# One group for both halves of the masked scores, context two steps behind, and turned weights on one queue: a cross-attention block on one core

## Chip, core and metric

The kernel runs on one core of one Trainium2 chip. The metric is device time in microseconds (us) of one execution, as the median of several runs. One further execution was taken by the hardware profiler; its rows are what "the profile" and "the trace" mean here. The engines are TensorE (PE: matmuls; PEld: its weight loads), VectorE (DVE), ScalarE (ACT), GpSimd (POOL) and SyncE (SP, which here only issues transfers). ACT can issue transfers too; "SPq" and "ACTq" are those issues.

## What is computed

A block of a transformer for 128 sequences of 128 tokens with 256 features, all in fp32: cross-attention with 16 heads of 16 features against a second input of the same shape, a layer norm, a feed-forward part of width 1024, and a second layer norm. The mask lets token i see only the tokens j < i of the other input; the first token sees none, and its attention is zero.

```python
q = (query @ Wq + bq).reshape(b, s, H, 16).transpose(0, 2, 1, 3)
k = (key @ Wk + bk).reshape(b, s, H, 16).transpose(0, 2, 1, 3)
v = (values @ Wv + bv).reshape(b, s, H, 16).transpose(0, 2, 1, 3)
scores = einsum('bhqd,bhkd->bhqk', q, k) / sqrt(16)
scores = where(j < i, scores, -1e30)
attn = softmax(scores, axis=-1)
attn = attn.at[:, :, 0, :].set(0.0)
ctx = einsum('bhqk,bhkd->bhqd', attn, v).transpose(0, 2, 1, 3).reshape(b, s, 256)
x = layer_norm(query + ctx @ Wo + bo, ln1_g, ln1_b)
out = layer_norm(x + relu(x @ W1 + b1) @ W2 + b2, ln2_g, ln2_b)
```

`query` is the input x; `key` and `values` are both the second input.

## The kernel before

The 128 sequences are worked in 64 pairs (`NP` = 64); one pair `p` is 256 columns in most matmuls. The order of the work on every engine is the order in which the program issues it: nothing reorders it. So `step(p)` (L821), which is called for p = 2 to 62, is the schedule, and what stands before it (prologue, pairs 0 and 1) and behind it (epilogue, from L934) are written out by hand. A wait arises where an instruction needs a result, or a buffer that another still reads.

**Stages of one pair.** `tokens` turns the loaded blocks into feature-major tiles `xT` and `cT` (VectorE). `queries`, `keys`, `values` are projections (TensorE) that ACT copies out of PSUM: `qT`, `kT`, and the values into `vz` and `vd`. ACT's `values_out` also issues one transfer that moves half of the values to other partitions of `vd`.

`scores(p, hi)` (L312) is done twice for a pair. The mask makes a triangle, so the last 64 queries of a sequence ("high", `hi` = 1) go against all 128 tokens and the first 64 ("low", `hi` = 0) only against the first 64. Each call is 32 matmuls on tiles of 32 rows (two heads) by 64 columns: four row strips `r` by two halves `s` (the two sequences). In both calls every row strip writes a PSUM bank of its own, `sps[r // 2][.., r % 2, ..]`.

`mask` (VectorE, out of PSUM), `maximum` (VectorE reduces, POOL subtracts), `exponential` (ACT) and `sums` (VectorE adds up and takes reciprocals, POOL multiplies) make the softmax: in two halves of the heads, `ONE` and `TWO`, for high and in one piece, `ALL`, for low. The weights must then be turned, tokens onto partitions: `turn` (L381) transposes 32x32 blocks on VectorE into `tb`, three calls a pair, and `bring` (L394) moves the blocks to their partitions by sixteen transfers into `pT`, one for each (i, j). In `step` eight are issued by SyncE, and eight by ACT between the relus of the hidden layer:

```python
def share(f):
    nonlocal at
    n = NS * NS - at if f == FC - 2 else 0 if f == 0 or p == 2 else NS // 2
    bring(p, nc.scalar, range(at, at + n))
    at += n
```

`weigh` (L424) multiplies `pT` with the values into `pc`, `context` (L454) copies `pc` to `cxT` on ACT, `attention_out` (L458) is the output projection `po`. `attention_sum`, `attention_stats`, `norm1` are the first layer norm; `turn_x1` turns its result, by a VectorE transpose, four transfers out to DRAM and one back in, all on SyncE. `hidden` (L639) makes `ph`, two chunks of 128 a bank, and ACT's relus write `hT`; `second` (L660) makes `py`. `second_sum`, `stats`, `scale_and_shift`, `norm2`, `finish` and `store` are the second layer norm and the way out.

**Order in a step.** TensorE does in step p: high scores of p, `second` of p−3, `weigh` of p−1, low scores of p, `queries(p+1)`, `attention_out(p-1)`, `keys(p+1)`, `values(p+1)`, `hidden(p-2)`. So the context of a pair is made one step behind its scores.

**PSUM.** Eight banks: `ps_2` holds two pairs of banks (used for scores only), `ps_1` four single banks that all else takes in turn through `bank` (L209).

**Ends.** For pairs 0, 1 and 63 the weights, and for pairs 0 and 63 `x1`, are turned by TensorE (`turn_on_pe`, L406; `turn_x1_on_pe`), with ACT copying out of PSUM.

Of the kernel before, what the change touches and what calls it, by code (L numbers as in the profile page):

```python
# [19 lines left out]
def tile_cross_attention_block(  # L20
# [51 lines left out]
    ps_2 = ctx.enter_context(tc.tile_pool(name="ps_2", bufs=2, space=bass.MemoryType.PSUM))  # L72
    ps_1 = ctx.enter_context(tc.tile_pool(name="ps_1", bufs=4, space=bass.MemoryType.PSUM))

# [132 lines left out]
    bov_r = const.tile([P, D], F32, tag="bov_r", name="bov_r")  # L207

    def bank(name):  # L209
        return ps_1.tile([P, 512], F32, tag="ps1", name=name)  # L210

# [39 lines left out]

    def project(w, src, name):
        ps = bank(name)
        for m in range(KC):
            for k in range(KC):
                nc.tensor.matmul(  # L256
                    ps[:, m * TP : (m + 1) * TP], w[:, k, m * P : (m + 1) * P], src[:, k, :],
                    start=(k == 0), stop=(k == KC - 1),
                )
        return ps  # L260

    def queries(p):
        st = states[p]
        st["qT"] = proj.tile([P, KC, TP], F32, tag="qT", name=f"qT_{p}")
        pq = project(wq, st["xT"], f"pq_{p}")
        for m in range(KC):
            nc.scalar.activation(
                st["qT"][:, m, :], pq[:, m * TP : (m + 1) * TP], AF.Identity,
                bias=bqs_c[:, m : m + 1], scale=QSCALE,
            )  # L270

    def keys(p):
        st = states[p]
        st["kT"] = proj.tile([P, KC, 2, TP], F32, tag="kT", name=f"kT_{p}")
        pk = project(wk, st["cT"], f"pk_{p}")
        for m in range(KC):
            for e in range(2):
                nc.scalar.activation(  # L278
                    st["kT"][:, m, e, :], pk[:, m * TP : (m + 1) * TP], AF.Identity,
                    bias=bkh[:, m, e : e + 1], scale=half[:, e : e + 1],  # L280
                )

    def values(p):
        st = states[p]
        pv = st["pv"] = bank(f"pv_{p}")
        for s in range(2):
# [25 lines left out]
    def scores(p, hi):  # L312
# [20 lines left out]
        )  # L333
        st["nmx", hi] = small.tile([P, H], F32, tag=f"nmx{hi}", name=f"nmx{hi}_{p}")

    def mask(p, hi, t):
# [87 lines left out]
    def weigh(p):  # L424

        st = states[p]
        pT = st.pop("pT")
        pc = bank(f"pc_{p}")

# [28 lines left out]
    def attention_out(p):  # L458
        st = states[p]
        po = st["po"] = bank(f"po_{p}")  # L460
        for s in range(2):
# [31 lines left out]
    def attention_stats(p):  # L493
        stats(p, states[p]["t1"], 1)
        deviation(p, 1)
# [143 lines left out]
    def hidden(p, fs, between=None):  # L639
        st = states[p]  # L640
        if fs[0] == 0:
            st["hT"] = ffn.tile([P, FC, TP], F32, tag="hT", name=f"hT_{p}")
        for f in fs[::2]:
            ph = bank(f"ph_{p}_{f}")
            for i in range(2):
# [14 lines left out]
    def second(p, s, fs=range(FC)):  # L660
        st = states[p]
        if s == 0 and fs[0] == 0:
            st["py"] = bank(f"py_{p}")
        for f in fs:
# [143 lines left out]
    def load_ahead(p):  # L808
        if p % 2 == 0 and p + 4 < NP:
            load([p + 4, p + 5], "x")  # L810
        if p % 2 == 1 and p + 3 < NP:
            load([p + 3, p + 4], "c")
            load_tokens((p + 3) // 2)

# [5 lines left out]

    def step(p):  # L821
        nonlocal waiting
        if p > 2:
            load_ahead(p)
        scores(p, 1)
        mask(p, 1, 0)
        maximum(p, 1, ONE)
        if p > 2:
            second(p - 3, 0)
            mask(p, 1, 1)  # L830
            maximum(p, 1, TWO)
            exponential(p, 1, ONE)
            second(p - 3, 1)
            if p + 2 < NP:
                tokens(p + 2, "c")
        else:
            turn_x1_on_pe(0)
            turn_on_pe(1, 1, range(2))
            fold_norm1()
            add_b1()  # L840
            hidden(0, range(FC // 4))
            mask(p, 1, 1)
            maximum(p, 1, TWO)
            exponential(p, 1, ONE)
            low_scores(p)
            hidden(0, range(FC // 4, FC // 2))
            turn_on_pe(1, 1, range(2, 4))
            turn_on_pe(1, 0, range(2))
            hidden(0, range(FC // 2, 3 * FC // 4))
            tokens(3, "x")  # L850
            add_bo(1)
        summed = []
        sums(p, 1, ONE)
        exponential(p, 1, TWO)
        if p > 2:
            second_sum(p - 3)
            summed = [p - 3]
        else:
            tokens(3, "c")
            load_ahead(2)  # L860
            load_tokens(2)
            exponential(p, 0, ALL)
        sums(p, 1, TWO)


        weigh(p - 1)
        context(p - 1)
        if p > 2:
            scores(p, 0)
        if p == 3:  # L870
            scale_w1()
            nc.gpsimd.tensor_tensor(b1e_c, b1e_c, b1_c, ALU.add)
        queries(p + 1)
        if p > 2:
            mask(p, 0, 0)
            mask(p, 0, 1)
            maximum(p, 0, ALL)
        if p > 2:
            exponential(p, 0, ALL)
        else:  # L880
            sums(p, 0, ALL)
            add_bo(2)
        turn(p, 1, 0)
        turn(p, 1, 1)
        for q in waiting:
            finish(q)
        attention_out(p - 1)
        attention_sum(p - 1)
        if p > 2:
            sums(p, 0, ALL)  # L890
        else:
            turn(p, 0, 0)
            bring(p, nc.sync, range(NS * NS // 2))
        attention_stats(p - 1)
        if p + 2 < NP:
            tokens(p + 2, "x")
            if p == 2:
                tokens(p + 2, "c")
        if p > 2:
            turn(p, 0, 0)  # L900
            bring(p, nc.sync, range(NS * NS // 2))
        keys(p + 1)
        norm1(p - 1)
        turn_x1(p - 1)
        values(p + 1)
        values_out(p + 1)
        for q in waiting:
            store(q)
        add_bo(p + 1)
        if p == 2:  # L910
            residual1(0)
        residual1(p - 1)
        for q in summed:
            stats(q, states[q]["t2"], 2)
        for q in summed:
            scale_and_shift(q)
        at = NS * NS // 2

        def share(f):
            nonlocal at  # L920
            n = NS * NS - at if f == FC - 2 else 0 if f == 0 or p == 2 else NS // 2
            bring(p, nc.scalar, range(at, at + n))
            at += n

        hidden(p - 2, range(0 if p > 2 else 3 * FC // 4, FC), share)
        for q in summed:
            norm2(q)
        waiting = summed

    waiting = []  # L930
    for p in range(2, NP - 1):
        step(p)

    p = NP - 1  # L934
    scores(p, 1)
    mask(p, 1, 0)
    maximum(p, 1, ONE)
    second(p - 3, 0)
    mask(p, 1, 1)
    maximum(p, 1, TWO)  # L940
    exponential(p, 1, ONE)
    second(p - 3, 1)
    sums(p, 1, ONE)
    exponential(p, 1, TWO)
    second_sum(p - 3)
    sums(p, 1, TWO)
    weigh(p - 1)
    context(p - 1)
    scores(p, 0)
    mask(p, 0, 0)  # L950
    mask(p, 0, 1)
    maximum(p, 0, ALL)
    hidden(p - 2, range(FC // 2))
    exponential(p, 0, ALL)
    finish(p - 4)
    attention_out(p - 1)
    attention_sum(p - 1)
    sums(p, 0, ALL)
    attention_stats(p - 1)
    norm1(p - 1)  # L960
    turn_x1(p - 1)
    store(p - 4)
    residual1(p - 1)
    stats(p - 3, states[p - 3]["t2"], 2)
    scale_and_shift(p - 3)
    hidden(p - 2, range(FC // 2, FC))
    turn_on_pe(p, 1, range(4))

    p = NP - 1
    turn_on_pe(p, 0, range(2))  # L970
    norm2(p - 3)
    finish(p - 3)
    second(p - 2, 0)
    weigh(p)
    context(p)
    second(p - 2, 1, range(FC // 2))
    store(p - 3)
    attention_out(p)
    second(p - 2, 1, range(FC // 2, FC))
    attention_sum(p)  # L980
    attention_stats(p)
    second_sum(p - 2)
    hidden(p - 1, range(FC - 2))
    norm1(p)
    stats(p - 2, states[p - 2]["t2"], 2)
    turn_x1_on_pe(p)
    hidden(p - 1, range(FC - 2, FC))
    residual1(p)
    scale_and_shift(p - 2)
    hidden(p, range(FC // 2))  # L990
    second(p - 1, 0)
    hidden(p, range(FC // 2, FC))
    norm2(p - 2)
    finish(p - 2)
    store(p - 2)
    second(p - 1, 1)
    second_sum(p - 1)
    stats(p - 1, states[p - 1]["t2"], 2)
    deviation(p - 1, 2)
# [6 lines left out]
    for s in range(2):  # L1006
        py = bank(f"py_last_{s}")
        for f in range(FC):
# [49 lines left out]
```

## Time and profile before

| what | value |
|---|---|
| median of 3 runs | 1588.46 us (1586.27 to 1589.66) |
| span of the profiled execution | 1585.6 us |
| TensorE busy | 1573.8 us, 16514 matmuls |
| VectorE busy | 1370.8 us |
| POOL busy | 1281.4 us |
| ACT busy | 757.5 us |
| granted TensorE clock, 71.21 to 1457.53 us | 1.00 |
| busy share of the 16 DMA engines, same stretch | 0.60 |

The span runs from the first to the last instruction of the profiled execution; the runs are timed from outside. Busy times of different engines overlap each other. Matmuls are pipelined, so in a timeline a group's duration reaches into the next line: the distance between two starts is what a group holds TensorE for. In a timeline row stand start, duration, engine, line, operation, the tile written, `<-`, the tiles read, the shape and how many instructions were joined (x32); in square brackets follows idle time of the engine ahead of it and what ended it.

### The profile page before, as it was taken

Reading aid. Unit: us, or ns where it says so; the run is one execution under the profiler, and the core shown is the slowest. Engines: PE = TensorE matmul, PEld = TensorE weight load, DVE = VectorE, ACT = ScalarE, POOL = GpSimd, SP = SyncE. Lnnn points to the kernel's source line nnn. Section 1 sums busy time; section 2 is a strip of 40 time slices with the busy share of each in tenths; the row PEclk is TensorE's granted clock in tenths of the full one; section 3 lists DMA queues with packets and bytes.
Section 4 is the critical chain, followed back from the end, with each engine's and each line's share of the span. In section 5 each row is a group of like instructions: output and inputs, shape, how many; then the busy total and the mean of one; then the engine's idle time right before and its main releaser. Section 6 shows DMA issues by size and latency. Waiting matters only on the chain.

```text
span 1585.6 us, 41282 instructions
## 1 busy us (share of the span) xinstructions
PE 1573.8 (99%) x16514; PEld 1326.7 (84%) x16514; DVE 1370.8 (86%) x1989; ACT 757.5 (48%) x1500; POOL 1281.4 (81%) x1105
## 2 busy tenths in 40 slices
PE   9999999999999999999999999999999999999998
PEld 7788888888888888888888888888888888888887
DVE  7898988888888988898898988888889889889872
ACT  5555454444444454444444544444444455445442
POOL 7888888788787888888888888888888888888883
PEclk9999999999999999999999999999999999999999
DMA  9565665655656556556566565565555665664521
GB/s 199 115 137 128 140 147 121 150 122 130 151 127 141 138 123 157 136 123 149 127 137 148 127 149 130 117 160 128 138 134 126 152 147 121 144 137 108 127 78 34
DMA packets 479935, 210.12 MB, mean 133 GB/s; under 512 B 348672, under 2 KB 448256, under 8 KB 479744
## 3 DMA queue, kind: packets, MB, share of 16 engines
q1 hardware_dynamic: 371104, 134.29, 39.1%
q10 hardware_dynamic: 108640, 73.19, 18.0%
q8 instruction: 131, 2.15, 0.6%
q14 instruction: 60, 0.49, 0.1%
HBM read 70.00 MB, written 33.03 MB: 65 GB/s over the span
## 4 chain that ended last, share of the span: by engine, by line
PE 91%; DVE 3%; DMA 2%; POOL 1%; SPq 1%; ACT 1%; issue 1%; ACTq 0%; POOLq 0%; DVEq 0%
PE ph L647 26%; PE py L665 26%; PE pq L256 7%; PE po L463 7%; PE pk L256 6%; PE pv L288 6%; PE pss L322 6%; PE pc L444 3%; PE pc L434 2%; DMA pT<-tb 2%; SPq L402 1%; DVE su L372 1%; POOL sm L374 1%; DVE tb L387 0%; POOL sm L353 0%
## 5 line engine op out<-in xcount | busy, mean ns | idle before, releaser
L353 POOL TENSOR_TENSOR sm<-sm,nmx 128x1024 f32<-128x1024 f32 x192 | 364.2, 1898 | 118.6 <-DVE nmx L352 118.4
L647 PE MATMUL ph<-x1T,w 128*128 128x256 f32 x2048 | 453.6, 379 | 0.0
L665 PE MATMUL py<-w,hT 128*128 128x256 f32 x2016 | 453.0, 382 | 0.1
L665 PEld LDWEIGHTS py<-w,hT 128*128 128x128 f32 x2016 | 377.5, 190 | 73.4 <-issue 18.1
L374 POOL TENSOR_TENSOR sm<-sm,rs 128x1024 f32<-128x1024 f32 x192 | 364.2, 1898 | 90.1 <-DVE rs L373 84.1
L647 PEld LDWEIGHTS ph<-x1T,w 128*128 128x128 f32 x2048 | 388.7, 190 | 53.5 <-ACT x1T L632 0.5
L653 ACT ACTIVATE hT<-ph,b1e_c 128x256 f32<-128x256 f32 x504 | 208.7, 471 | 205.1 <-PE ph L647 99.2
L360 ACT ACTIVATE sm<-sm 128x1024 f32<-128x1024 f32 x192 | 201.1, 1054 | 203.9 <-POOL sm L353 195.6
L372 DVE TENSOR_REDUCE su<-sm 128x8 f32<-128x1024 f32 (+1 forms) x192 | 233.7, 1217 | 68.8 <-ACT sm L360 66.5
L341 DVE TENSOR_TENSOR sm<-pss,neg 128x1024 f32<-128x1024 f32 (+1 forms) x256 | 235.2, 940 | 51.1 <-PE pss L322 51.1
L387 DVE STREAM_TRANSPOSE tb<-sm 128x1024 f32<-128x1024 f32 x183 | 219.9, 1227 | 27.8 <-POOL sm L374 27.8
L352 DVE TENSOR_REDUCE nmx<-sm 128x8 f32<-128x1024 f32 (+1 forms) x192 | 234.3, 1220 | 6.6
L542 ACT ACTIVATE t<-t,nb,sd 128x256 f32<-128x256 f32 x124 | 67.7, 593 | 188.5 <-DMA pT<-tb 106.6
L256 PE MATMUL pq<-xT,wq 128*128 128x256 f32 x504 | 125.5, 392 | 0.0
L278 ACT ACTIVATE kT<-pk,bkh,half 128x256 f32<-128x256 f32 x252 | 120.6, 558 | 3.9 <-PE pk L256 3.8
L463 PE MATMUL po<-wo,cxT 128*128 128x256 f32 x512 | 121.1, 379 | 0.0
L288 PE MATMUL pv<-wv,cT 128*128 128x256 f32 x512 | 121.0, 379 | 0.0
L256 PE MATMUL pk<-cT,wk 128*128 128x256 f32 x504 | 119.2, 379 | 0.0
L322 PE MATMUL pss<-kT,qT 32*64 32x256 f32 (+1 forms) x4096 | 116.7, 334 | 0.0
L517 POOL TENSOR_TENSOR x1b<-x,g_r 128x512 f32<-128x512 f32 x64 | 81.5, 1273 | 34.9 <-DVE x L509 34.9
L463 PEld LDWEIGHTS po<-wo,cxT 128*128 128x128 f32 x512 | 97.2, 190 | 13.5 <-ACT cxT L456 0.3
L288 PEld LDWEIGHTS pv<-wv,cT 128*128 128x128 f32 x512 | 97.2, 190 | 13.2
(99 smaller groups left out, 1716.1 us busy)
## 6 DMA issues: line engine op xcount, KB each, us to landing
pT<-tb SPq DMA_DIRECT2D x488, 96.0 KB, 3.0
pT<-tb ACTq DMA_DIRECT2D x488, 96.0 KB, 2.7
out_dram<-t ACTq DMA_DIRECT2D x63, 256.0 KB, 2.5
xb<-in_x_dram SPq DMA_DIRECT2D x124, 128.0 KB, 4.5
cb<-in_ctx_dram SPq DMA_DIRECT2D x124, 128.0 KB, 4.3
x<-in_x_dram SPq DMA_DIRECT2D x31, 512.0 KB, 5.0
x1t<-tbx SPq DMA_DIRECT2D x248, 64.0 KB, 2.3
x1T<-x1t SPq DMA_DIRECT2D x62, 256.0 KB, 3.2
```

The lines of the kernel that those rows point to most:

```text
L256: nc.tensor.matmul(ps[:, m * TP : (m + 1) * TP], w[:, k, m * P : (m + 1) * P], src[:, k, :], start=(k == 0), stop=(k == KC - 1),)
L288: nc.tensor.matmul(pv[:, s * D : (s + 1) * D], st["cT"][:, k, s * P : (s + 1) * P], wv[:, k, :], start=(k == 0), stop=(k == KC - 1),)
L322: nc.tensor.matmul(sps[r // 2][s * HP : (s + 1) * HP, r % 2, m * 2 * n : (m + 1) * 2 * n].rearrange("p (e j) -> p e j", e=2), st["qT"][str ...
L341: nc.vector.tensor_tensor(st["sm", hi][:, part, :].rearrange("p (r n) j -> p r n j", r=2), st["sps", hi][t][:, :, : 4 * n].rearrange("p r ...
L352: nc.vector.tensor_reduce(nmx[:, part], sm[:, part, :], AX.X, ALU.max, negate=True)
L353: nc.gpsimd.tensor_tensor(sm[:, part, :], sm[:, part, :], nmx[:, part, None].to_broadcast([P, part.stop - part.start, n]), ALU.add,)
L372: nc.vector.tensor_reduce(su, sm[:, part, :], AX.X, ALU.add)
L374: nc.gpsimd.tensor_tensor(sm[:, part, :], sm[:, part, :], rs[:, :, None].to_broadcast([P, part.stop - part.start, n]), ALU.mult,)
L387: nc.vector.transpose(st["tb"][:, :, at : at + 256].rearrange("p j (n a) -> p n j a", a=32), st["sm", hi].rearrange("p h j -> p (h j)")[:, ...
L463: nc.tensor.matmul(po[:, s * D : (s + 1) * D], cxT[:, k, s, :], wo[:, k, :], start=(k == 0), stop=(k == KC - 1),)
L647: nc.tensor.matmul(ph[:, i * TP : (i + 1) * TP].rearrange("p (s i a) -> p s i a", s=2, a=32), w1[:, k, (f + i) * P : (f + i + 1) * P], st[ ...
L665: nc.tensor.matmul(st["py"][:, s * D : (s + 1) * D], st["hT"][:, f, s * P : (s + 1) * P], w2[:, f, :], start=(f == 0), stop=(f == FC - 1),)
```

## The change

High and low scores of a pair are issued together, in `scores_both`: eight groups of four tiles, with the low scores in one fixed pair of banks, `low`. Strips 0 and 1 share the first of them and strips 2 and 3 the second, at different offsets; `one` and `two` take the strips of a bank in opposite halves of the partitions. Ahead of the last eight low matmuls stands a tiny ACT copy from `low` into `hop`. `mask_low` masks all low scores in one instruction. The other single banks shrink to two; `queries`, `weigh` and `attention_out` use those, `second` too, `keys` and `values` share a pair, `hidden` takes a pair for its first half and `low` for its second. `hT` has one buffer instead of two.

In the new `step(p)`, called for p = 4 to 63, TensorE does `weigh(p-2)`, both scores of p, `queries(p+1)`, `attention_out(p-2)`, `keys(p+1)`, `values(p)`, `hidden(p-3)`, `second(p-3)`. The context is made two steps behind the scores. The sixteen transfers of `bring(p-1)` are all issued by SyncE, in one run. `third` and `fourth` are the steps for p = 2 and 3 (`fourth` weighs nothing); the last step issues half of `bring(62)` from ACT, and in the epilogue pair 63 is turned by `turn` and `bring` and `turn_x1` as the others are, not by TensorE.

```diff
-    ps_1 = ctx.enter_context(tc.tile_pool(name="ps_1", bufs=4, space=bass.MemoryType.PSUM))
+    ps_1 = ctx.enter_context(tc.tile_pool(name="ps_1", bufs=2, space=bass.MemoryType.PSUM))
+    ps_l = ctx.enter_context(tc.tile_pool(name="ps_l", bufs=1, space=bass.MemoryType.PSUM))
...
+    low = ps_l.tile([P, 2, 512], F32, tag="low", name="low")
+    turns = [0]
+
+    def single(name):
+        return ps_1.tile([P, 512], F32, tag="ps1", name=name)
+
     def bank(name):
-        return ps_1.tile([P, 512], F32, tag="ps1", name=name)
+        turns[0] += 1
+        return single(name) if turns[0] % 4 < 2 else low[:, turns[0] % 2]
...
+    hop = const.tile([HP, 2, 1], F32, tag="hop", name="hop")
+
+    def scores_both(p):
+
+        st = states[p]
+        sps = [pair(f"pss_{p}_{t}") for t in range(2)]
+        one = [(1, 1), (3, 1), (0, 0), (2, 0)]
+        two = [(1, 0), (0, 1), (3, 0), (2, 1)]
+        for tiles, hi, m in (
+            (one, 0, 0), (two, 1, 0), (one, 0, 1), (one, 1, 0),
+            (two, 1, 1), (one, 1, 1), (two, 0, 0), (two, 0, 1),
+        ):
+            n = P if hi else HP
+            for r, s in tiles:
+                strip, first = slice(32 * r, 32 * r + 32), s * P
+                rows = slice(s * HP, (s + 1) * HP)
+                at = m * 2 * n
+                if hi:
+                    to = sps[r // 2][rows, r % 2, at : at + 2 * n]
+                else:
+                    to = low[rows, r // 2, r % 2 * 4 * n + at : r % 2 * 4 * n + at + 2 * n]
+                nc.tensor.matmul(
+                    to.rearrange("p (e j) -> p e j", e=2),
+                    st["qT"][strip, m, first + hi * HP : first + hi * HP + HP],
+                    st["kT"][strip, m, :, first : first + n],
+                    start=True, stop=True,
+                )
+            if not hi and tiles is one and m == KC - 1:
+                nc.scalar.copy(hop, low[:HP, :, 2 * n : 2 * n + 1])
...
+    def mask_low(p):
+        nc.vector.tensor_tensor(
+            states[p]["sm", 0],
+            low.rearrange("p b (n j) -> p (b n) j", j=HP),
+            neg[:, 1, None, :].to_broadcast([P, H, HP]),
+            ALU.add,
+        )
...
-            st["hT"] = ffn.tile([P, FC, TP], F32, tag="hT", name=f"hT_{p}")
+            st["hT"] = ffn.tile([P, FC, TP], F32, tag="hT", name=f"hT_{p}", bufs=1)
         for f in fs[::2]:
-            ph = bank(f"ph_{p}_{f}")
+            if p == 0:
+                ph = bank(f"ph_{p}_{f}")
+            elif f < FC // 2:
+                if f == 0:
+                    st["ph"] = pair(f"ph_{p}")
+                ph = st["ph"][:, f // 2]
+            else:
+                ph = low[:, f // 2 - 2]
...
+    EVERY = range(NS * NS)
...
+    def fourth():
+        p = 3
+        load_ahead(p)
+        scores_both(p)
+        mask(p, 1, 0)
+        maximum(p, 1, ONE)
+        second(0, 0)
+        exponential(p, 1, ONE)
+        mask(p, 1, 1)
+        maximum(p, 1, TWO)
+        second(0, 1)
+        scale_w1()
+        mask_low(p)
+        maximum(p, 0, ALL)
+        queries(p + 1)
+        exponential(p, 1, TWO)
...
+        keys(p + 1)
+        second_sum(0)
...
+    def step(p):
+        last = p == NP - 1
+        load_ahead(p)
+        weigh(p - 2)
+        scores_both(p)
+        context(p - 2)
+        if p > 4:
+            second_sum(p - 4)
+        turn(p - 1, 1, 0)
+        turn(p - 1, 1, 1)
+        if p > 4:
+            residual1(p - 3)
+            finish(p - 5)
+            add_bo(p - 1)
+        mask(p, 1, 0)
+        maximum(p, 1, ONE)
+        if not last:
+            queries(p + 1)
+        if p > 4:
+            store(p - 5)
+        attention_out(p - 2)
+        mask(p, 1, 1)
+        maximum(p, 1, TWO)
+        exponential(p, 1, ONE)
+        turn(p - 1, 0, 0)
+        bring(p - 1, nc.sync, EVERY[: 8 if last else 16])
+        mask_low(p)
+        maximum(p, 0, ALL)
+        if not last:
+            keys(p + 1)
+        else:
+            bring(p - 1, nc.scalar, EVERY[8:])
+            states[p]["pkv"] = pair(f"pkv_{p}")
+        exponential(p, 1, TWO)
+        attention_sum(p - 2)
+        stats(p - 4, states[p - 4]["t2"], 2)
+        scale_and_shift(p - 4)
+        values(p)
+        values_out(p)
+        sums(p, 1, ONE)
+        exponential(p, 0, ALL)
+        attention_stats(p - 2)
+        sums(p, 1, TWO)
+        hidden(p - 3, range(FC))
+        norm2(p - 4)
+        sums(p, 0, ALL)
+        norm1(p - 2)
+        turn_x1(p - 2)
+        if p + 2 < NP:
+            tokens(p + 2, "x")
+            tokens(p + 2, "c")
+        second(p - 3, 0)
+        second(p - 3, 1)
+
+    third()
+    fourth()
+    for p in range(4, NP):
+        step(p)
     p = NP - 1
...
     weigh(p - 1)
     context(p - 1)
...
+    turn(p, 1, 0)
+    turn(p, 1, 1)
+    turn(p, 0, 0)
+    bring(p, nc.sync, EVERY[:8])
...
+    bring(p, nc.scalar, EVERY[8:12])
...
+    hidden(p - 2, range(FC // 2))
+    bring(p, nc.scalar, EVERY[12:])
...
-    turn_on_pe(p, 1, range(4))
...
-    turn_on_pe(p, 0, range(2))
...
-    turn_x1_on_pe(p)
...
+    turn_x1(p)
```

## The prediction

> **What bounds the kernel now.** I read the page from the top: busy shares, then the chain that ended last.
>
> ```profile
> PE 1573.8 (99%) x16514; PEld 1326.7 (84%) x16514; DVE 1370.8 (86%) x1989; ACT 757.5 (48%) x1500; POOL 1281.4 (81%) x1105
> PE 91%; DVE 3%; DMA 2%; POOL 1%; SPq 1%; ACT 1%; issue 1%; ACTq 0%; POOLq 0%; DVEq 0%
> ```
>
> TensorE is busy for 99% of the span and carries 91% of the chain. Between 71.21 and 1457.53 us it is busy 1385.01 of 1386.32 us. A change pays only by taking time from TensorE's own stream; a wait anywhere else that reaches TensorE costs in full. So next the timeline of TensorE for one pair (start, duration, operation, count).
>
> ```profile
> 760.16 7.07 PE L647 MATMUL ph<-x1T,w 128*128 128x256 f32 x32
> 767.16 1.12 PE L322 MATMUL pss<-kT,qT 32*64 32x256 f32 x32
> 768.21 7.17 PE L665 MATMUL py<-w,hT 128*128 128x256 f32 x32
> 775.31 0.43 PE L434 MATMUL pc<-pT,vd 128*32 128x64 f32 x16
> ...
> 776.79 0.69 PE L322 MATMUL pss<-kT,qT 32*64 32x128 f32 x32
> 777.41 1.99 PE L256 MATMUL pq<-xT,wq 128*128 128x256 f32 x8
> 779.25 1.89 PE L463 MATMUL po<-wo,cxT 128*128 128x256 f32 x8
> 780.97 1.89 PE L256 MATMUL pk<-cT,wk 128*128 128x256 f32 x8
> 782.70 1.89 PE L288 MATMUL pv<-wv,cT 128*128 128x256 f32 x8
> 784.42 7.07 PE L647 MATMUL ph<-x1T,w 128*128 128x256 f32 x32
> ```
>
> Starts are what to compare, since a duration overlaps the next line. One pair takes 784.42 − 760.16 = 24.26 us. High scores hold 768.21 − 767.16 = 1.05 and low scores 777.41 − 776.79 = 0.62, at two separate places.
>
> **The merged scores.** Eight plain 128x256 matmuls take 782.70 − 780.97 = 1.73, so 32 take 6.91. The 32 of ph, which end at scores, take 7.00; the 32 of py, which begin after scores and end at pc, take 7.10; pq, after scores, takes 1.84. Each change of tile shape therefore costs about 0.09 going out and 0.10 coming in. Today's step has four such changes from plain to narrow and back: into and out of high scores, into pc, and out of low scores. After the change pc and scores stand together: two remain.
> Inside a group, 32 matmuls of 256 columns take 1.05 and 32 of 128 columns 0.62. If a + 2b = 1.05 and a + b = 0.62, then b = 0.43 and a = 0.19 is a fixed part. One group of both is a + 3b = 1.48.
> New in it is `hop`, an ACT copy that the last eight low matmuls wait for. The twelve high matmuls behind the first low ones cover 12 × 1.05 / 32 = 0.39. PE to ACT takes 0.14 (pc ends 776.79, the context copy starts 776.93), the nearest small copy is 0.36 (L303), and the way back I estimate at 0.1: the copy itself is far smaller, so between 0.39 and 0.60 in all, a wait of 0 to 0.2. I take 0.1, so 1.58.
> New step: ph 6.91, py 7.00 (out into pc 0.09), pc 776.79 − 775.31 = 1.48, scores 1.58, pq 1.84, po, pk, pv 784.42 − 779.25 = 5.17; the sum is 23.98. That is −0.28 a step (−0.38 with hop free), for the 61 pairs from 3 to 63: **−17.1 us**.
>
> [...] In every row here each 32-row strip of scores writes a bank of its own; after, strips 0 and 1 write halves of one bank, and so do 2 and 3, so no row here prices it. [...] I take none, as the tiles write disjoint halves and the low group of today runs eight tiles the same way.
>
> **What feeds TensorE.** Weighing of pair p−2 opens step p, so the turned weights must have landed within one step of their high part. That loop decides. The rows for its links (VectorE's and SyncE's timelines):
>
> ```profile
> 768.35 1.22 DVE L341 TENSOR_TENSOR sm<-pss,neg 128x1024 f32<-128x1024 f32 x1 [1.15 <-PE pss L322]
> 775.42 0.69 DVE L673 TENSOR_TENSOR t<-py,x1b 128x512 f32<-128x512 f32 x1
> 780.10 2.36 DVE L387 STREAM_TRANSPOSE tb<-sm 128x1024 f32<-128x1024 f32 x2
> 786.87 1.25 DVE L387 STREAM_TRANSPOSE tb<-sm 128x1024 f32<-128x1024 f32 x1 [0.46 <-POOL sm L374]
> ...
> 763.93 5.01 SPq L402 DMA_DIRECT2D pT<-tb  x8
> ...
> 83.27 6.40 SPq L402 DMA_DIRECT2D pT<-tb  x8
> ```
>
> From the step's start: 0.1 from py's end, second_sum 0.69, two turns 2.36: 3.15, when scores (1.48 + 1.58 = 3.06) are ready. Mask, maximum, mask, maximum run 768.35 to 773.13, 4.78: 7.93. The low turn 1.22: 9.15. Then SyncE issues all sixteen transfers, where it issues eight today: at 5.01 / 8 = 0.63 the sixteenth starts at 9.15 + 15 × 0.63 = 18.6 and lands, 3.0 us later by the page, at 21.6. TensorE asks at 23.98: slack 2.4. In the built order, in every other step one of the sixteen, the eighth at the earliest (13.6), also waits for ACT's vd transfer. That lands at about 15.0: the second maximum 7.93, POOL's subtraction 1.90, the exponential 1.06, two vz copies 0.65, the issue 0.67, landing 2.8. So up to 1.4 more: 23.0, slack 1.0. I cost the move at **0**, covered by that slack; past it every microsecond is paid in each step.
> Moved past on SyncE: x1t's four issues (2.14) with x1T (0.38), and the loads' 3.18 to 3.6 behind them. The queue is busy for 10.1 + 2.5 + 3.4 = 16 of 24 us. x1T lands after about 18.7 + 2.5 + 3.2 plus its wait, early in the next step, and is read at 10.1 there: hidden.
> ACT loses eight issues and gains hop: relief. VectorE has 21.70 busy of 24.26 today; one 128x1024 mask (1.22) replaces two halves (1.24 together): nothing. POOL, 20.04 a step, does the same work in new order: nothing, cover 3.9. hT with one buffer: the relus of pair p−3 begin after py of p−4 is read, which is the step before: nothing.
>
> [...]
>
> **The ends.** ACT's queue in the prologue, then TensorE's next stall; last two transposes of the epilogue.
>
> ```profile
> 60.32 4.47 ACTq L402 DMA_DIRECT2D pT<-tb  x7
> ...
> 69.09 0.46 PE L434 MATMUL pc<-pT,vd 128*32 128x64 f32 x16 [1.35 <-DMA pT<-tb]
> ...
> 1539.06 2.78 PE L417 MATMUL ptp<-ident,sm 128*128 128x128 f32 x24
> ...
> 1557.19 0.60 PE L222 MATMUL ptn<-ident,x 128*128 128x128 f32 x4
> ```
>
> - Pair 3: scores start at 59.51 and hop is queued on ACT behind bring(2)'s eight issues, which end at 60.32 + 4.47 = 64.8. TensorE waits from about 61 to 65.1: +4.0, less today's 1.35 stall, which that hides: +2.6. The key projection's copies follow late: +1.0. Bounds 0 and 6.
> - Step 63 alone issues half of bring(62) from ACT, ahead of its exponentials and relus: eight issues of 0.64 hold ACT for 5.1, and the hidden layer's banks wait for relus: +4.9 (bounds 0 and 5.1).
> - Epilogue: 24 + 4 transposes go, 1541.68 − 1539.06 + 1557.63 − 1557.19 = −3.06; two context copies stand bare (each 0.14 + 0.58 + about 0.1): +1.6.
>
> Sum: −17.1 + 3.6 + 4.9 − 1.5 = −10.1. The profiled span 1585.6 becomes 1575.5; the median of the runs lies 2.9 above that span, so **1578**. With each bound taken its best way the sum is −23.2 − 1.5, so 1564; its worst, hop at 0.2, −11.0 + 6 + 5.1 − 1.5, so 1587 (low scores at double time are left to rival D).
>
> **Rivals.**
> - *B, the saving is eaten.* Hop's round trip costs 0.3 or more beyond its cover, so a step gains 0.1: −6 + 7 = +1: 1589. For it: no row shows such a round trip inside a group. Against: context copy starts 0.14 after PE. Chance 0.12.
> - *C, slower: SyncE's sixteen issues become the bound.* Place: weighing at the start of each step, waiting on pT. It decides from an issue spacing of 0.72: 9.15 + 10.8 + 3.0 = 22.95 and, in every other step, 24.35. At 0.78 these are 23.85 and 25.25, a mean step of (23.98 + 25.25) / 2 = 24.62: 59 × 0.36 + 6 = +27: 1616. At 0.80 both kinds wait (24.15, 25.55): 1630. For it: 6.40 / 8 = 0.80 already occurs at 83.27. Against: 0.63 in the steady step, at the same 16 engines' load. Chance 0.20.
> - *D, the mixed order does not run eight tiles at a time*, or halves of one bank collide: +0.43 a step undoes the gain and more: 61 × (0.43 − 0.28) + 7 = +16: 1605; if the whole group halves in speed (+1.5), 61 × 1.2 + 7 = +81: 1670. For it: only the uniform orders are seen in rows. Chance 0.08.
>
> **How the numbers follow.** The forecast has 0.60, its own range 1564 to 1587. A measurement of this kernel can tell about 0.2%, 3.2 us, so faster is below 1585.3, same to 1591.6. Faster: 0.58 of the forecast, 0.03 of B, 0.01 of C: 0.62. Same: 0.02, 0.06, 0.02: 0.10. Slower: the rest, 0.28. The range reaches up to 1610, into half of C and D, and down to 1565; about 0.2 stays outside.
>
> **What would show it.** Right: score groups of some 1.5 to 1.6 from start to start once a step, a step of 24.0, no TensorE wait on pT, SyncE's issue run x16 near 10.1. Hop too dear: a gap ahead of the last eight score matmuls. C: idle time before weighing, released by the pT transfers. D: the score group well over 1.7 with no wait. The ends: a TensorE stall near 61 and another near the last step, put down to ACT. I would be wrong if POOL's or VectorE's new order made queries or scores wait, which I costed at nothing.

## The result, and the profile after

The changed kernel takes 1995.91 us (median; 1992.39 to 2003.31 in 4 runs) against 1588.86 us of the kernel before on the same chip: a ratio of 1.2576 (95% interval 1.2549 to 1.2603). The forecast was 1578 us, with a range from 1565 to 1610. The page of the changed kernel, its span, busy times and shares of the chain that ended last:

```profile
span 1993.2 us, 41338 instructions
...
PE 1681.2 (84%) x16486; PEld 1382.7 (69%) x16486; DVE 1476.6 (74%) x1932; ACT 752.5 (38%) x1553; POOL 1279.5 (64%) x1105
...
PE 37%; DVE 32%; ACT 11%; DMA 8%; issue 5%; SPq 3%; POOL 2%; ACTq 1%; DVEq 0%; POOLq 0%
```

TensorE is no longer the whole chain: its share falls from 91% to 37%, and it idles for 312 us where it idled for 12. The timeline of TensorE for one step (start, duration, work, in brackets the wait; of the scores only the first row) shows where:

```profile
952.31 0.43 PE L489 MATMUL pc<-pT,vd 128*32 128x64 f32 x16
...
953.79 0.34 PE L368 MATMUL low<-kT,qT 32*64 32x128 f32 x4
...
955.41 1.99 PE L263 MATMUL pq<-xT,wq 128*128 128x256 f32 x8
957.24 1.89 PE L518 MATMUL po<-wo,cxT 128*128 128x256 f32 x8
958.97 1.89 PE L263 MATMUL pkv<-cT,wk 128*128 128x256 f32 x8
962.88 1.99 PE L299 MATMUL pkv<-wv,cT 128*128 128x256 f32 x8 [2.02 <-ACT kT L289]
964.72 1.89 PE L709 MATMUL ph<-x1T,w 128*128 128x256 f32 x8
968.33 1.99 PE L709 MATMUL ph<-x1T,w 128*128 128x256 f32 x8 [1.73 <-ACT hT L715]
970.16 1.89 PE L709 MATMUL low<-x1T,w 128*128 128x256 f32 x8
972.98 1.99 PE L709 MATMUL low<-x1T,w 128*128 128x256 f32 x8 [0.93 <-ACT hT L715]
974.81 7.07 PE L727 MATMUL py<-w,hT 128*128 128x256 f32 x32
981.81 0.43 PE L489 MATMUL pc<-pT,vd 128*32 128x64 f32 x16
```

The step takes 29.50 us. In each of three places TensorE is about to write one bank of a two-bank tile while ACT still has to read the other: values behind the copies of keys (both `pkv`), the second bank of `ph` behind the relus of the first, the second bank of `low` likewise. Nothing that is read is overwritten, since values, say, go to `both[:, 1]` while ACT reads `both[:, 0]`. The program waits all the same: its waits seem to go by tile and not by bank, which the first experiment tests. ACT's timeline in the same step gives the other end of each wait:

```profile
960.90 1.93 ACT L289 ACTIVATE kT<-pkv,bkh,half 128x256 f32<-128x256 f32 x4
...
966.50 1.05 ACT L415 ACTIVATE sm<-sm 128x1024 f32<-128x1024 f32 x1
967.46 0.82 ACT L715 ACTIVATE hT<-ph,b1e_c 128x256 f32<-128x256 f32 x2
...
972.09 0.84 ACT L715 ACTIVATE hT<-low,b1e_c 128x256 f32<-128x256 f32 x2 [0.89 <-PE low L709]
```

The keys' copies end at 962.83 and values start at 962.88; the relus end at 968.28 and `ph` goes on at 968.33; 972.93 and 972.98. The relus are themselves late, behind the low exponential (966.50). Summed over the run, from the view of waits (engine, line, releaser: us in total, times, longest):

```profile
PE pkv L299 <- ACT kT L289: 120.5, 59, 3.2
PE ph L709 <- ACT hT L715: 97.9, 63, 11.0
PE low L709 <- ACT hT L715: 58.9, 64, 0.9
```

That is 277 us of waiting. The longest wait, 11.0 us, is in the last step, where ACT has eight transfers to issue ahead of the relus. Most steps are longer than 29.50, though, up to 32.4 ahead of the last. In windows of the step before (busy us of PE, PEld, DVE, ACT, POOL, then granted clock, DMA share, GB/s) the clock shows why:

```profile
932.50:935.00 2.50, 2.50 (x9) 2.10 (x10) 2.43 (x7) 0.89 (x1) 1.56 (x1) 0.74 0.64 155
935.00:939.00 4.00, 3.07 (x10) 2.19 (x9) 3.86 (x10) 2.81 (x6) 3.72 (x7) 0.73 0.45 94
939.00:943.00 4.00, 3.55 (x16) 2.79 (x16) 3.97 (x4) 1.25 (x4) 3.92 (x4) 1.00 0.55 131
```

About 1.2 us behind the end of the wait on keys the granted clock falls to 0.50, for 3.41 us (933.71 to 937.12); such a stretch is called a dip below. In that time matmuls of 256 columns start 0.427 us apart instead of 0.216. Over the run some 290 matmuls do, which is 61 us more. Waits and dips give 338 us of 407. Besides, each wait holds TensorE for longer than its idle time: from 958.97 to 962.88 are 3.91 us, 2.18 above the normal 1.73, of which 2.02 show as idle, and from 962.88 to 964.72 are 1.84. The ends are longer too; on the other side stands the gain of the merge. Counted by steps, the 57 intervals between weighings in the middle of the run (all 63 but the first four and the last two) take 30.48 us on the mean and 24.32 before, which is 351 us; the other 56 us lie in the prologue, the last steps and the epilogue.

### The profile page after: what moved, and what is told of

The parts are those of the page before. It is cut to its first block, busy times and chain, and to the rows that moved or that the text cites. A ratio compares the mean times of both kernels' runs of the same rounds, so it can differ in the third digit from the quotient of the medians.

```text
span 1993.2 us, 41338 instructions
## 1 busy us (share of the span) xinstructions
PE 1681.2 (84%) x16486; PEld 1382.7 (69%) x16486; DVE 1476.6 (74%) x1932; ACT 752.5 (38%) x1553; POOL 1279.5 (64%) x1105
## 4 chain that ended last, share of the span: by engine, by line
PE 37%; DVE 32%; ACT 11%; DMA 8%; issue 5%; SPq 3%; POOL 2%; ACTq 1%; DVEq 0%; POOLq 0%
PE py L727 13%; PE low L709 7%; DVE tb L442 6%; DVE x L564 5%; DVE nmx L407 5%; DVE sm L396 5%; PE ph L709 5%; DVE su L427 5%; PE pkv L299 4%; ACT kT L289 3%; ACT hT L715 3%; ACT sm L415 3%; DMA x1t<-tbx 3%; DMA cb<-in_ctx_dram 2%; DMA xb<-in_x_dram 2%
## 5 line engine op out<-in xcount | busy, mean ns | idle before, releaser
L709 PE MATMUL ph<-x1T,w 128*128 128x256 f32 x1016 | 271.7, 414 | 97.9 <-ACT hT L715 97.9
L709 PEld LDWEIGHTS ph<-x1T,w 128*128 128x128 f32 x1016 | 210.7, 212 | 157.8 <-ACT hT L715 123.1
L709 PE MATMUL low<-x1T,w 128*128 128x256 f32 x1032 | 253.5, 389 | 58.9 <-ACT hT L715 58.9
L709 PEld LDWEIGHTS low<-x1T,w 128*128 128x128 f32 x1032 | 193.2, 192 | 109.6 <-ACT hT L715 84.4
L299 PE MATMUL pkv<-wv,cT 128*128 128x256 f32 x480 | 160.6, 493 | 120.5 <-ACT kT L289 120.5
L564 DVE TENSOR_SCALAR x<-t,mv,sd 128x256 f32<-128x256 f32 x126 | 222.8, 1808 | 0.2
L299 PEld LDWEIGHTS pkv<-wv,cT 128*128 128x128 f32 x480 | 107.9, 235 | 161.6 <-ACT kT L289 144.2
L715 ACT ACTIVATE hT<-low,b1e_c 128x256 f32<-128x256 f32 x252 | 105.8, 471 | 189.0 <-PE low L709 187.0
L375 ACT COPY hop<-low 64x2 f32<-64x2 f32 x61 | 9.4, 153 | 436.1 <-PE low L368 430.6
L715 ACT ACTIVATE hT<-ph,b1e_c 128x256 f32<-128x256 f32 x252 | 104.8, 466 | 150.4 <-PE ph L709 145.0
L603 POOL TENSOR_TENSOR t<-t,g_r 128x512 f32<-128x512 f32 x62 | 78.6, 1268 | 71.3 <-ACT t L597 71.1
```

The lines of the kernel that those rows point to most:

```text
L299: nc.tensor.matmul(pv[:, s * D : (s + 1) * D], st["cT"][:, k, s * P : (s + 1) * P], wv[:, k, :], start=(k == 0), stop=(k == KC - 1),)
L564: nc.vector.tensor_scalar(x1[:, s], t1[:, s], mv[:, s, 0:1], sd[:, s], ALU.subtract, ALU.mult)
L709: nc.tensor.matmul(ph[:, i * TP : (i + 1) * TP].rearrange("p (s i a) -> p s i a", s=2, a=32), w1[:, k, (f + i) * P : (f + i + 1) * P], st[ ...
L715: nc.scalar.activation(st["hT"][:, f + i, :], ph[:, i * TP : (i + 1) * TP], AF.Relu, bias=(b1e_c if p else b1_c)[:, f + i : f + i + 1], sc ...
```

## Experiments

All ratios are to the kernel before, run beside each.

**One tile for each bank.**

```diff
-        return ps_2.tile([P, 2, 512], F32, tag="ps2", name=name)
+        return [ps_2.tile([P, 512], F32, tag="ps2", name=f"{name}_{b}") for b in range(2)]
...
-    low = ps_l.tile([P, 2, 512], F32, tag="low", name="low")
+    low = [ps_l.tile([P, 512], F32, tag=f"low{b}", name=f"low{b}") for b in range(2)]
...
-                nc.scalar.copy(hop, low[:HP, :, 2 * n : 2 * n + 1])
+                for b in range(2):
+                    nc.scalar.copy(hop[:, b], low[b][:HP, 2 * n : 2 * n + 1])
```

> Every two-bank PSUM tile becomes two tiles of one bank (scores, keys and values, hidden, the shared low banks); masks take two instructions of 128x512 for one of 128x1024, hop is copied from each low bank. Theory W: the 400 us are TensorE writes to one half of a two-bank tile that wait until ACT has read the other half (2.2 us ahead of values, 1.9 ahead of the second hidden bank, 1.1 ahead of the last, of 29.50 in a step at full clock) and the clock dips behind these waits (0.9 us in steps of 30.39). With them gone a step takes 24.0 to 24.8 and the run 1575 to 1625 us. Rival S: SyncE's sixteen issues, 12 to 13 us a step, set the step; then 1950 or more. Rival V: VectorE, 23.3 us busy a step, with its place behind second_sum sets it; then no gain, as this kernel adds instructions to it.

Measured: 1593.23 us, ratio 1.0038 (1.0024 to 1.0052). Order, banks and queues are as in the changed kernel (the masks and `hop` now go bank by bank); 403 us are gone. TensorE in one step of it:

```profile
758.46 0.43 PE L492 MATMUL pc<-pT,vd 128*32 128x64 f32 x16
...
761.59 1.99 PE L263 MATMUL pq<-xT,wq 128*128 128x256 f32 x8
763.42 1.89 PE L521 MATMUL po<-wo,cxT 128*128 128x256 f32 x8
765.14 1.89 PE L263 MATMUL pkv<-cT,wk 128*128 128x256 f32 x8
766.87 1.89 PE L299 MATMUL pkv<-wv,cT 128*128 128x256 f32 x8
768.60 3.62 PE L712 MATMUL ph<-x1T,w 128*128 128x256 f32 x16
772.05 3.62 PE L712 MATMUL low<-x1T,w 128*128 128x256 f32 x16
775.50 7.07 PE L730 MATMUL py<-w,hT 128*128 128x256 f32 x32
782.50 0.43 PE L492 MATMUL pc<-pT,vd 128*32 128x64 f32 x16
```

No wait is left in this step, and it takes 782.50 − 758.46 = 24.04 us, as do 49 of the 63 intervals between weighings. With that the rivals, SyncE or VectorE as the bound of the changed kernel's step, fall. The lower half of the expected range was missed: the ends, and some longer steps, keep it at 1593.

**Keys in a bank of their own, alone.**

```diff
-            pk = project(wk, st["cT"], both[:, 0])
+            pk = project(wk, st["cT"], single(f"pk_{p}"))
```

> Only the keys' projection goes to a single bank, so values need not wait for the copies of keys; hidden keeps its pairs. Theory W: the wait ahead of values (2.2 us) goes, but the second hidden bank then waits longer, since the relus stand behind the low exponential on ACT, which ends about 14.5 us into the step whatever TensorE does: 0.6 us a step saved, 1960 us or so. If each wait counted by itself: 2.2 x 59 = 130 us, 1866.

Measured: 1996.36 us, ratio 1.2573 (1.2548 to 1.2598): nothing gained. TensorE's rows:

```profile
957.38 1.89 PE L299 MATMUL pkv<-wv,cT 128*128 128x256 f32 x8
959.11 1.89 PE L709 MATMUL ph<-x1T,w 128*128 128x256 f32 x8
964.29 2.83 PE L709 MATMUL ph<-x1T,w 128*128 128x256 f32 x8 [3.29 <-ACT hT L715]
```

The wait of 2.02 is gone and the next is 3.29 instead of 1.73: the relus end when the exponential ahead of them lets them. Steps at full clock are 28.77 us, 0.73 shorter, about as worked out; but the longer wait is followed by a dip nearly every time (`ph` starts at 964.29 and the next row 2.62 later, not 1.73), and most steps are 30.45. The mean of the 57 steps in the middle is 30.42, against 30.48 in the changed kernel. The dips, which I had not priced, ate the gain.

**The hidden layer's banks taken in turn from two tiles, alone.**

```diff
+    MIXED = [0, 1, 4, 5, 2, 3, 6, 7]
...
-        hidden(p - 3, range(FC))
+        hidden(p - 3, MIXED)
```

> Only the order of the hidden layer's banks changes: pair 0, low 0, pair 1, low 1 in place of pair 0, pair 1, low 0, low 1, so that a bank of the other tile lies between the two of one tile. Theory W: the two hidden waits (1.9 and 1.1 us) are covered by 1.73 us of matmuls each: 3 us a step, 1996 - 180 = 1815 us. If the sharing of tiles isn't it: no change.

Measured: 1816.3 us, ratio 1.1439 (1.1401 to 1.1477), on the expected figure. The waits of the two rows below were 97.9 and 58.9 us in the changed kernel, while that of values stays at 120.5:

```profile
PE ph L709 <- ACT hT L715: 12.9, 5, 8.4
PE low L709 <- ACT hT L715: 3.9, 4, 1.7
```

The mean of the 57 steps falls from 30.48 to 27.44 us, by the 3 us of the theory.

**Both edits.**

> Both of the two edits before. Theory W: values go at once, the first two hidden banks are done 13.6 us into the step, the third waits for the first relu at 15.4, behind the low exponential: a step of 25.5 to 25.8, 1995 - 59 x 5 = 1700 us.

Measured: 1730.19 us, ratio 1.0897 (1.0875 to 1.0919), a steady step of 25.85 us. That is 30 us above the expected figure: 4.6 us came off the mean step, not 5. The one wait that stays, on TensorE, and ACT's rows ahead of it:

```profile
841.10 1.99 PE L709 MATMUL ph<-x1T,w 128*128 128x256 f32 x8 [1.56 <-ACT hT L715]
```

```profile
839.26 1.06 ACT L415 ACTIVATE sm<-sm 128x1024 f32<-128x1024 f32 x1 [0.41 <-POOL sm L408]
840.22 0.82 ACT L715 ACTIVATE hT<-ph,b1e_c 128x256 f32<-128x256 f32 x2
```

Together the two edits bring 266 us, apart 0 and 180.

**The relus ahead of the low exponential.** On top of both edits:

```diff
-        exponential(p, 0, ALL)
         attention_stats(p - 2)
         sums(p, 1, TWO)
-        hidden(p - 3, MIXED)
+        hidden(p - 3, MIXED, lambda f: exponential(p, 0, ALL) if f == 4 else None)
```

> e4 (two-bank tiles kept, keys apart, hidden banks alternating), with the low exponential moved on ACT from ahead of the relus to behind the first four. Theory: what keeps e4's step at 25.85 us and not 24.04 is the 1.56 us that the third hidden bank waits for the first relu, which stands behind that exponential: 0.3 to 0.5 us stay, a step of 24.3 to 24.5, 1730 - 59 x 1.45 = 1645 us. If something else holds that step: no change. If the exponential, now 1.2 us later, holds up VectorE: in between.

Measured: 1641.02 us, ratio 1.034 (1.0321 to 1.0359), most steps from 24.37 to 24.45. The order on ACT was the cause of nearly all that was left in the step. Of the 48 us above the kernel of one-bank tiles, the mean step, longer by 0.31, makes 18; by the two traces the other 30 lie at the ends: the first weighing comes 7.6 us later, the next four intervals are 8.4 longer together, the last two 9.5, and what follows 4.8.

**Only the wait ahead of values.** The counterpart of the second experiment: `low` as two tiles, the first half of the hidden layer in single banks, keys and values in one tile as in the change.

```diff
-                if f == 0:
-                    st["ph"] = pair(f"ph_{p}")
-                ph = st["ph"][:, f // 2]
+                ph = single(f"ph_{p}_{f}")
...
-                ph = low[:, f // 2 - 2]
+                ph = low[f // 2 - 2]
```

> The counterpart of e2: of the two-bank tiles only that of keys and values keeps its wait; low is two tiles and the hidden layer's first half takes single banks (scores keep their pairs, which only VectorE reads). If the wait ahead of values is worth what it shows, 2.2 us a step, and nothing else covers it now: steps of 26.2, 1593 + 59 x 2.2 = 1723 us, and up to 3.1 us a step, 1776, where the clock dips behind it. If e2 showed that this wait is worth nothing: 1620 or less.

Measured: 1778.51 us, ratio 1.1205 (1.1151 to 1.1259): 185 us above the kernel without any of the waits, for a wait whose removal had brought nothing, and just above the dearer of the two expected figures. TensorE in two steps of it:

```profile
858.35 3.42 PE L299 MATMUL pkv<-wv,cT 128*128 128x256 f32 x8 [2.02 <-ACT kT L289]
861.56 3.92 PE L709 MATMUL ph<-x1T,w 128*128 128x256 f32 x16
...
886.37 1.99 PE L299 MATMUL pkv<-wv,cT 128*128 128x256 f32 x8 [2.02 <-ACT kT L289]
888.20 3.62 PE L709 MATMUL ph<-x1T,w 128*128 128x256 f32 x16
```

The same wait of 2.02 us: values then hold TensorE for 3.21 us in one step and 1.83 in the next. Steps are 26.33 or 28.02.

**The ends.** On the kernel of one-bank tiles: in `fourth`, `bring(2, nc.scalar, EVERY[8:])` now follows `scores_both`, so that it stands behind `hop`; in the last step SyncE issues all sixteen.

```diff
-        hidden(0, range(3 * FC // 4, FC), lambda f: bring(p, nc.scalar, EVERY[8:]))
+        hidden(0, range(3 * FC // 4, FC))
...
         scores_both(p)
+        bring(2, nc.scalar, EVERY[8:])
...
-        bring(p - 1, nc.sync, EVERY[: 8 if last else 16])
+        bring(p - 1, nc.sync, EVERY)
```

> The kernel of one-bank tiles (e1) with two ends mended: ACT issues its half of the weights of pair 2 behind hop and not ahead of it, and SyncE alone issues those of pair 62. Theory: what keeps e1 above the forecast of 1578 are the ends, as its trace shows 3.0 us of waiting on hop with 1.7 us of half clock behind it, and 5.0 us in the last step: 1593.2 - 9.7 = 1583.5 us, a ratio of 0.997 to before. Rival: VectorE, busy 23.5 of 24.04 us a step, makes up for it elsewhere; then 1590 or more.

Measured: 1588.49 us, ratio 1.001 (1.0002 to 1.0019); half of what was expected. In the prologue the interval between two weighings falls from 28.86 to 24.25 us, as it should. The last step falls from 29.06 to 22.22, but the next interval rises from 17.99 to 24.84:

```profile
1526.80 1.99 PE L521 MATMUL po<-wo,cxT 128*128 128x256 f32 x8 [0.70 <-ACT cxT L514]
1533.70 5.41 PE L712 MATMUL ph<-x1T,w 128*128 128x256 f32 x16 [4.90 <-DMA x1T<-x1t]
```

The stall in the last step had hidden that pair 61 is normalised late; what was won there is waited for here.

**Pair 61 earlier.** In the last step `norm1` and `turn_x1` go ahead of the last two sums.

```diff
+        if last:
+            norm1(p - 2)
+            turn_x1(p - 2)
         sums(p, 1, TWO)
...
-        norm1(p - 2)
-        turn_x1(p - 2)
+        if not last:
+            norm1(p - 2)
+            turn_x1(p - 2)
```

> e5, with norm1 and turn_x1 of pair 61 ahead of the last two sums of the last step. Theory: e5 gave back in the epilogue (4.9 us of waiting on x1T of pair 61, 24.84 us between the last two weighings against 17.99 in e1) what it won in the last step, because x1T stands behind 2.7 us of sums on VectorE and a norm1 of 3.8 us; three to five microseconds come back, 1584 us, a ratio of 0.997 to before. Rival: the sums, now later, make the turned weights of pair 63 late instead; then 1588 as before.

Measured: 1582.84 us (1580.82 to 1584.70, 10 runs), ratio 0.997 (0.996 to 0.9979). This version beats the kernel before by 0.3%: little, but no run of the one overlaps with a run of the other (1585.43 to 1589.34 beside it). The interval behind the last step is 18.95 us.

**norm1 at the start of a step.**

```diff
         context(p - 2)
         if p > 4:
+            norm1(p - 3)
+            turn_x1(p - 3)
             second_sum(p - 4)
...
-        norm1(p - 2)
-        turn_x1(p - 2)
+        if last:
+            norm1(p - 2)
+            turn_x1(p - 2)
```

> e5, with norm1 and turn_x1 of a pair moved from the end of a step to the start of the next, ahead of second_sum, where POOL stands idle (some 3.6 us a step in e1). In e1 the two norm1 instructions take 3.78 us beside POOL's multiplications, 0.73 in the epilogue where POOL does nothing. Theory: two instructions of VectorE at the same time as POOL's big ones cost 3 us of VectorE a step; here they take 0.7 to 1.6, VectorE's busy time falls by 2 to 3 us a step, and only the stray stalls (3 us over the run) can be gained, 1580 to 1584. Rival: the later x1T or the later masks make TensorE wait: 1590 or more.

Measured: 1612.9 us, ratio 1.0146 (1.0124 to 1.0167). The rival's figure came true, its reason only in part. The instructions got cheaper by less than thought (mean 1333 ns, 1853 in the kernel of one-bank tiles). TensorE waits on `x1T`, whose transfers stand behind the loads on SyncE, nine times (8.9 us), but 4.6 of that is behind the last step, where the version of the ends waits too (4.9). So 4 us are new, of 18 between the two profiles. Other steps are longer by up to 2.4 us; the cause stays open.

**Half of the transfers back on ACT.** On the version of the ends, two transfers behind each hidden bank's relus.

```diff
-        bring(p - 1, nc.sync, EVERY)
+        bring(p - 1, nc.sync, EVERY if last else EVERY[:8])
...
-        hidden(p - 3, range(FC))
+        hidden(p - 3, range(FC), None if last else lambda f: bring(p - 1, nc.scalar, EVERY[8 + f : 10 + f]))
```

> e5, but in every step except the last only eight of the sixteen transfers of turned weights are issued by SyncE and eight by ACT, two behind each hidden bank's relus, as in the kernel before. Theory: moving them to SyncE cost nothing, since the weights land before they are asked for: within 3 us of e5. Rival S: the sixteen issues on one queue are what e5's steps wait for now and then: then a gain of 3 us or more.

Measured: 1903.03 us, ratio 1.1985 (1.1963 to 1.2007). Neither theory allowed for that. ACT's queue, then SyncE's:

```profile
915.78 0.84 ACT L718 ACTIVATE hT<-low,b1e_c 128x256 f32<-128x256 f32 x2 [0.45 <-issue]
922.89 1.16 ACTq L460 DMA_DIRECT2D pT<-tb  x2
```

```profile
920.78 1.76 SPq L241 DMA_DIRECT2D x1t<-tbx  x4
```

The last two issues come 6 us after the relus and TensorE waits for them 58 times, 3.5 us on the average. The trace names the semaphore of each transfer: there are eight for all queues together, with 217 or 218 transfers on each, here as in the changed kernel. In the changed kernel's trace the landing of the transfer before on the same semaphore stands for 1516 issues: none of them begins ahead of it, and 67 begin less than 0.05 us behind it, the nearest 0.016. Here ACT's seventh shares with the second of `x1t`, which SyncE issues at 921.14; that lands at 922.87, and ACT issues at 922.89. These waits are 204 us of the 315 above the version of the ends; behind them the clock dips (granted clock 0.931 over the run, 0.998 there), which I take for most of the rest. So the move to SyncE was free in this order, and undoing it was not.

## Why the prediction was wrong

- *The step that failed: "po, pk, pv 784.42 − 779.25 = 5.17" and "ph 6.91", taken over into the new step's sum.* Those rows are of a kernel in which each of these results has a bank that is a tile of its own. The change puts keys with values, and the hidden layer's banks two by two, into one tile each, so that TensorE waits for ACT's reads of one bank before it writes the other. I listed that move in the change and put it at nothing without a reason. In a step at full clock it costs 29.50 − 24.04 = 5.46 us: idle 2.02 ahead of values, 1.73 and 0.93 ahead of the second bank of `ph` and of `low`, the rest in stopping and starting. With the dips that follow and the ends it is worth 403 us (the first experiment).
- *The merged scores.* The term held, though its 0.1 for hop did not rest on rows alone: the way back from ACT was a bare estimate of 0.1, and the three waits above end 0.05 behind ACT (962.83 to 962.88, say); hop itself takes 0.15 (L375, 61 times) where 0.36 was the nearest. From pc to pq the changed kernel takes 955.41 − 952.31 = 3.10 us, of which 1.48 is pc and 1.62 the group, against 1.58; the step without the waits is 24.04 against 23.98, in the kernel of one-bank tiles. The gain is real, 24.26 − 24.04 = 0.22 us a step.
- *Row strips in one bank.* The cost that was weighed did not come: the group would have taken about 2.0 us with the low scores at double time, and took 1.62. What it takes above 1.48 may be `hop` or the mixed order; no run parts them. That eight tiles run at a time in the low group of before is an estimate from its rows: 32 plain matmuls of 128 columns would take 32 × 0.108 = 3.46 us, eight times the 0.43. That strips in one bank cost nothing is shown for this layout alone, where the strips of a bank write opposite halves of the partitions and `hop` parts the two rounds. Without `hop` it wasn't tried.
- *The loop through SyncE.* Costed at nothing, and right, but partly by luck: in the kernel of one-bank tiles TensorE waits on `pT` once, 1.7 us, for pair 3. The sixteen issues did not take 10.1 us. In the step shown above they begin 9.28 us behind its start (forecast 9.15):

```profile
767.74 12.27 SPq L460 DMA_DIRECT2D pT<-tb  x16
```

Over the 57 steps in the middle the issues are 0.72 us apart (median; 0.63 in the sum), which is where rival C begins, and the sixteenth starts at 20.1 and not at 18.6. But it lands 2.1 us later and not 3.0, so that the weights are there at 22.3 of 24.04 us (median), between the 21.6 and the 23.0 of the prediction. Two wrong terms made up for each other, and rival C did not come. The wait on the landing of ACT's `vd` transfer, put in every other step, stands in nearly every step of the changed kernel: by turns the eighth or the tenth of the sixteen begins 0.016 or 0.017 us behind that landing (58 waits, 158.8 us on SyncE's queue).
- *hT with one buffer, POOL, VectorE: nothing.* No wait was put down to them, but VectorE's cover was thinner than I had it: norm1 takes 3.8 us a pair and not 1.6, so it is busy 23.5 us of 24.04.
- *The ends.* In the kernel of one-bank tiles the last step costs 29.06 − 24.04 = 5.0 us (forecast 4.9); pair 3's wait on hop is 3.0, with 1.7 us of half clock behind it that I did not count; in the changed kernel and in this one the two bare context copies cost 0.70 and 0.76 (0.8 each). The kernel of one-bank tiles is 15 us above the forecast: 3.5 from the step's 0.06, about 3 more of stray stalls than before, and the rest at the ends.
- *Rivals.* None of them named the mechanism that came.

## What to carry to other kernels

Where a change packs results that are written and read at different times into one tile, read in the built program what the first write to each half waits for before any row is carried over to the new schedule: here the wait went with the tile, and one tile for each bank took 403 us away. A wait is priced by what else would hold the work behind it, and by the dip that may follow: the one ahead of values was worth nothing with the hidden waits behind it, and 185 us without them. And an end that is cut short should be followed to the next wait on the same chain, since a stall hides whatever is later than it needs to be.

## What the runs showed of the hardware

*The clock behind short waits.* In the experiment with the one wait ahead of values, waits of 2.02 us were followed by a half clock in some steps (28.02 us) and not in others (26.33). The windows view of that run (`low` as two tiles, only values wait), TensorE alone, with stretches of 3.41 us laid against the dip at 858.75:

```profile
855.34:858.75 3.41, 1.39 (x7) 1.00 0.12 29
858.75:862.17 3.42, 3.42 (x10) 0.50 0.67 160
...
882.64:886.05 3.41, 1.70 (x8) 1.00 0.04 14
886.05:889.47 3.42, 3.10 (x14) 1.00 0.64 155
```

The dip fills one stretch. In the first step the whole wait lies in the stretch ahead of it (TensorE idle for 2.02 of 3.41 us); in the second a border cuts the wait into 1.71 and 0.32, and no dip follows. From 60 us on, all dips of this run, and all of the changed kernel, start a multiple of one such stretch of 3.41 us apart. In the changed kernel 43 of 563 stretches are followed by half clock: 42 of them have 2.02 us of idle time or more, the other is itself at half clock; the 520 that are not have 1.93 or less. In this run 32 of 34 have 2.02 or more (the two others 1.73 and 1.40), and the rest 1.98 or less. So in these two runs the place of a short wait on this grid decides, but for three of the 77 stretches ahead of half clock, and the border lies near 2.0 us idle of 3.41. A stretch need not be idle as a whole: 2.0 us were enough.

*VectorE beside POOL.* The two norm1 instructions of a pair take as long as the POOL multiplications that start with them; VectorE's row and POOL's row of the changed kernel, and VectorE's in the epilogue of the kernel of one-bank tiles, where POOL has only small instructions (0.22 and 0.71 us):

```profile
970.43 3.77 DVE L564 TENSOR_SCALAR x<-t,mv,sd 128x256 f32<-128x256 f32 x2
```

```profile
970.25 3.80 POOL L429 TENSOR_TENSOR sm<-sm,rs 128x1024 f32<-128x1024 f32 x2
```

```profile
1560.94 0.73 DVE L567 TENSOR_SCALAR x<-t,mv,sd 128x256 f32<-128x256 f32 x2
```

Each of the two instructions takes as long as one multiplication: 1.9 us where 0.37 would do. Of the 126 in the changed kernel, 121 have POOL instructions of over 1 us beside them for more than half of their time: their median is 1.87 us, and the other five take 0.32 to 0.41. Over the run these instructions take 222.8 us in the changed kernel and 100.4 before. The rows show that the long ones stand beside POOL's long ones, not by what means.
